# In the steps that clear the bank of sums, the sums go behind the step's other products in TensorE's order

## The chip, the cores and the metric

The kernel runs on one core of a Trainium2 chip. The metric is the device time of one execution in microseconds (us). Before the change three runs took 12238.09, 12265.75 and 12289.24 us; their median is 12265.75 us.

## The reference

Two layers of the same kind follow each other on 8 images of 64 x 64 positions and 96 channels. Each layer normalises its input by groups of three channels, projects it to 192 inner channels, applies a 3 x 3 convolution to each channel and a SiLU, and then runs a state-space scan over the positions in four directions: by rows, by columns, and both backwards. In a direction every channel has 16 states, driven by a step width delta:

```python
dA = jnp.exp(d_t[..., None] * A)
h = dA * h + d_t[..., None] * B_e * u_t[..., None]
return (h, jnp.sum(h * C_e, axis=-1))
```

The four directions are summed, normalised over the channels, gated with a SiLU of a second projection, projected back to 96 channels and added to the layer's input. The second layer writes the same scan with cumulative sums.

## The kernel before

**Tiling of the scan.** The scan of one image is cut into units (4 directions x 4 pieces of 1024 positions), a unit into two jobs (halves of 96 channels), a job into three groups of 32 channels, and a group into four sets of four states, so that a set fills 128 partitions x 1024 positions. One image has 384 such sets, and the main loop of `scan_rows` (L431) goes through them one set a step; each step `n` issues pieces of the work of several sets, ahead of it and behind it. For the second layer most of the scan is left out, and six short sets at the end of an image's loop stand for it. Between the loops of two images stands an output phase.

**One set.** ScalarE (ACT) computes the decay into one of two PSUM tiles (`fill`, L936). VectorE (DVE) multiplies the drive with B (L970) and runs the scan in place (L983). For the last set of each group GpSimd (POOL) makes that product in DVE's place (`early`, L960). POOL multiplies the scanned states with C (`read_out`, L999) into one of four `out` buffers. TensorE (PE) sums the states of each channel (`collect`, L1035): eight matmuls with a 0/1 matrix, which add into the group's bank `acc`. There is one bank, `pacc` having one buffer. For the first set of a group `collect` first clears the bank: it starts the accumulation with the sum so far, read from the map (L1026, eight matmuls), and then adds the eight products. When the fourth set of the group is in, ACT copies the bank back to the map in four pieces (`release`, L1065).

**The order in a step.** The whole loop is under `manual_schedule`, so each engine runs its instructions in the order in which the code emits them. In step `n` the loop emits `advance_set` for set `n`, `keep_state` for `n - 1`, `fill` for `n + 1`, `drive`, `release` for set `n - 4`, `read_out` for set `n - 1`, `early` for set `n + 2`, `collect` for set `n - 3`, and at last the stages that the plan holds for this step. The buffer that `collect` has read in step `n` is written again by the read-out of step `n + 2`. In every fourth step, where `n + 1` is a multiple of 4, `release` empties the bank of one group and `collect` clears it for the next.

**The plan.** It is a dictionary from steps to lists of stages, filled with fixed offsets. A job's offsets count from the step `n = 12 m - 1`, so offsets 0, 4, 8 and 12 fall on the steps that clear the bank. Two users share one PSUM bank, `pmisc`, with a single buffer:

- `ready_by_time` (L673) prepares the step widths delta of the job two ahead: `argument(0)` at offset 0 and `argument(1)` at offset 1 (L690, eight matmuls each, with 7 rows), taken by ACT with `parts` (L701, L702) at offsets 1 and 2; elementwise work at offsets 3 to 7; `total` at offsets 10 and 11 (L724), taken by ACT with `delta` (L736) at offsets 11 and 12; POOL's `product` (L602) at 13, and the stores to DRAM at 14. Offset 12 of one job is offset 0 of the next: there `delta(1)` empties the bank that `argument(0)` takes.
- `conv_beside` (L1068 and on) convolves the next image's maps, one window of 8 rows and 96 channels in a job. `products` (L1102) adds 9 taps, each a pair of matmuls; then ACT's tanh (`curve`, L1112), DVE's `product` (L1115) and a store follow. `windows` (L1163) gives the start and the counts of taps in successive steps: (3, 2, 2, 2) from offset 3 in most jobs, with the tanh at offset 7 and the product at 9; (3, 3, 3) from offset 5 in jobs that also project; (3, 3, 3) from offset 10 in the last two jobs of an image.
- `projection` (L563) of a unit two ahead has its matmuls (L572) at offsets 2 and 3, in every second job of the first two directions.

```python
release(at(-4), y, beside)
gate(at(1))
read_out(at(-1), work)
early(at(2), work)
collect(at(-3), xc, y, pacc)
for stage in plan.pop(n, []):
    stage()
```

Of the kernel before, what the change touches and what calls it, by code (L numbers as in the profile page):

```python
# [29 lines left out]
NS = N // GS  # L30
# [22 lines left out]
def two_ss2d_layers(ctx: ExitStack, tc: tile.TileContext, t: dict, out: bass.AP):  # L53
# [377 lines left out]
    def scan_rows(xc, y, parts, plan, rows, beside):  # L431

        with (
            tc.tile_pool(name="loads", bufs=2, side="right") as loads,
            tc.tile_pool(name="piece", bufs=1) as piece,
            tc.tile_pool(name="work", bufs=2) as work,
            tc.tile_pool(name="pslot", bufs=2, space=PSUM) as pslot,
            tc.tile_pool(name="pdrive", bufs=1, space=PSUM) as pdrive,
            tc.tile_pool(name="pacc", bufs=1, space=PSUM) as pacc,
            tc.tile_pool(name="pmisc", bufs=1, space=PSUM) as pmisc,
        ):  # L450
            units, jobs, sets, x_dbl = parts
            total = len(sets)
            plan = plan(pmisc)
            with tc.manual_schedule():
                state = None
                arena = piece.tile([P, 4 * T], F32, name="arena")
                plan.setdefault(-1, []).insert(0, lambda: low_rows(x_dbl, units[1], rows))
                for n in range(-AHEAD, max(total + 4, max(plan, default=0) + 1)):
                    at = lambda i: sets[n + i] if 0 <= n + i < total else None
                    m, j = divmod(n + 1, PER)  # L460
                    if j == 0 and 0 <= m < len(jobs):

                        stages = []
                        if m + 2 < len(jobs):
                            prepare = short_ready if jobs[m + 2]["unit"]["short"] else ready_by_time
                            stages += prepare(xc, x_dbl, jobs[m + 2], arena, pmisc)
                        if m % NH == 1 and m // NH + 2 < len(units):
                            unit = units[m // NH + 2]
                            project = short_projection if unit["short"] else projection
                            stages += project(xc, x_dbl, unit, rows, pmisc)  # L470
                        for step, stage in stages:
                            plan.setdefault(n + step, []).append(stage)
                    fetch(at(AHEAD), False, loads)
                    fetch(at(2), True, loads)
                    replicate(at(AHEAD_BC), x_dbl, loads)
                    replicate_short(at(AHEAD_BC), "b", loads)
                    replicate_short(at(AHEAD_BC - 1), "c", loads)
                    if at(0) and at(0)["unit"]["nth"] == 0 and at(0)["first"]:
                        state = piece.tile([P, D // GC * NS], F32, name="state0", bufs=2)
                    advance_set(at(0), state, work)  # L480
                    keep_state(at(-1))
                    fill(at(1), pslot)
                    drive(at(2), False, pdrive)
                    drive(at(1), True, pdrive)
                    release(at(-4), y, beside)
                    gate(at(1))
                    read_out(at(-1), work)
                    early(at(2), work)
                    collect(at(-3), xc, y, pacc)
                    for stage in plan.pop(n, []):  # L490
                        stage()
                assert not plan

    def blocks(ap, i):
# [24 lines left out]
    def fetch(s, short, loads):  # L519

        if s and s["i"] == 0 and s["unit"]["short"] == short:
            group, n = s["group"], s["unit"]["n"]
            for c in ("dt", "dtu", "cum") if short else ("dt", "dtu"):
                if c == "cum":
                    rep = loads.tile([P, T], F32, tag="bc_rep", name="cum_rep", bufs=ring(s))
                else:
                    rep = loads.tile([P, T], F32, name=f"{c}_rep")
                group[c] = rep[:, :n]
                src = group["job"][f"{c}_far"][GC * group["g"] :, :][:GC, :]
                nc.sync.dma_start(group[c], src.unsqueeze(1).broadcast_to([GC, GS, n]))  # L530

    def replicate(s, x_dbl, loads):

        if s and s["group"]["h"] == 0 and s["group"]["g"] == 0 and not s["unit"]["short"]:
            unit = s["unit"]
            rows = x_dbl[unit["k"] % 2][unit["k"] // 2 * ROWS :, unit["t0"] : unit["t0"] + T]
            for c, at in (("b", R + 1), ("c", R + 1 + N)):
                rep = loads.tile([P, T], F32, tag="bc_rep", name=f"{c}_rep", bufs=2 * NS + 1)
                src = rows[at + GS * s["i"] :, :][:GS, :]
                nc.sync.dma_start(rep, src.unsqueeze(0).broadcast_to([GC, GS, T]))  # L540
                unit[c, s["i"]] = rep

    def replicate_short(s, c, loads):

        if s and s["unit"]["short"] and s["group"]["h"] == 0 and s["group"]["g"] == 0:
            unit = s["unit"]
            rep = loads.tile([P, T], F32, tag="bc_rep", name=f"{c}_rep", bufs=ring(s))
            unit[c, 0] = rep[:, :HT]
            at = R if c == "b" else R + N
            for i in range(NS):  # L550
                src = blocks(unit["far"][at + GS * i :, :][:GS, :], i)
                nc.sync.dma_start(
                    blocks(unit[c, 0], i), src.unsqueeze(0).broadcast_to([GC, *src.shape])
                )

    def low_rows(x_dbl, unit, piece):

        k, t0 = unit["k"], unit["t0"]
        unit["x_dbl"] = piece.tile([2 * ROWS, T], F32, name="x_dbl0")
        src = x_dbl[k % 2][k // 2 * ROWS :, t0 : t0 + T]  # L560
        nc.sync.dma_start(unit["x_dbl"][: R + 1, :], src[: R + 1, :])
# [387 lines left out]
    def drive(s, short, pdrive):  # L949

        if s and s["i"] == 0 and s["unit"]["short"] == short:
            s["group"]["drive"] = pdrive.tile([P, T], F32, name="drive")[:, : s["unit"]["n"]]
            nc.scalar.copy(s["group"]["drive"], s["group"]["dtu"])  # L953
# [38 lines left out]
    def keep_state(s):  # L992
        if s and not s["unit"]["short"] and s["unit"]["nth"] < NT - 1:
            nc.scalar.copy(s["last"], s["buf"][:, edge(s["unit"])])  # L994
# [6 lines left out]
    def collect(s, xc, y, pacc):  # L1001

        if not s:
            return
        unit, group = s["unit"], s["group"]
        h, g = group["h"], group["g"]
        if s["i"] == 0:
            group["acc"] = pacc.tile([P, MM], F32, name="acc0")
        if unit["short"]:
            for k in range(K):  # L1010
                for i in range(NS):
                    nc.tensor.matmul(  # L1012
                        group["acc"][GC * k : GC * (k + 1), head_of(i, k)],
                        w["gather"],
                        s["out"][:, place(i, k)],
                        start=i == 0,
                        stop=i == NS - 1,
                        skip_group_check=True,
                    )
            return  # L1020
        n = T // Q
        parts = [(group["acc"][GC * a : GC * (a + 1), :n], a * n) for a in range(Q)]
        if s["i"] == 0:
            old, lhs = (xc, w["skip0"][:, h, :]) if unit["k"] == 0 else (y, w["eye"])
            for acc, at in parts:
                nc.tensor.matmul(  # L1026
                    acc,
                    lhs[:, GC * g : GC * (g + 1)],
                    positions(old[:, h, :], unit["column"], unit["t0"] + at, n),
                    start=True,  # L1030
                    stop=False,
                    skip_group_check=True,
                )
        for acc, at in parts:
            nc.tensor.matmul(  # L1035
                acc,
                w["gather"],
                s["out"][:, at : at + n],
                start=False,
                stop=s["i"] == NS - 1,  # L1040
                skip_group_check=True,
            )
# [854 lines left out]
    xc, parts = begin()  # L1897

    with tc.manual_schedule():
        for b in range(NB):  # L1900
            y = keep.tile([C, NH, L], F32, name="map")
# [5 lines left out]
            if b + 1 < NB:  # L1907
                xc, parts = between(b, y)
# [101 lines left out]
```

## Time and profile before

| | |
|---|---|
| profiled execution | 12297.89 us, its span 12296.1 us |
| median of three runs | 12265.75 us |
| mean granted TensorE clock | 0.767 |
| collect L1035, PE | 24576 matmuls, 512 ns mean, 2447.3 us busy |
| clearing L1026, PE | 4608 and 1536 matmuls, 588 and 505 ns; idle before them 1681.6 and 288.3 us |
| release L1065, ACT | 3072 copies, 478 ns |
| taps L1102, PE | 4032 matmuls, 741 ns |
| argument L690, PE | 3840 matmuls, 353 ns |
| delta L736, ACT | 480 copies, 582 ns |
| tanh L1112, ACT | 224, 594 ns; idle before them 278.6 us |
| read-out L999, POOL | 3120, 2364 ns; idle before them 926.3 us |
| scan L983, DVE | 2304 and 768, 2344 and 2285 ns |

The profile is of one execution. "Idle before" is the time in which the engine did nothing directly ahead of the instructions of a row, and the releaser is what ended that time. Matmuls are pipelined, so that the mean length of one is longer than the time that each adds to the engine; the busy sums do not count the overlap twice. In the timeline a row merges equal instructions that follow closely (x8), with the start of the first and the time from there to the end of the last.

### The profile page before, as it was taken

To read this page: it belongs to the slowest core of one execution; us is meant where nothing else is said; L and a number is where in the kernel's file an instruction comes from. 1 tells how busy PE (TensorE), PEld (TensorE's weight loads), DVE (VectorE), ACT (ScalarE), POOL (GpSimd) and SP (SyncE) were. 2 spreads that over 40 slices of the span, in tenths; PEclk is the share of its full clock that TensorE was granted. 3 is DMA by queue.
4 is the path that set the end of the run, shared out by engine and by line. 5 is a ranking of instruction groups with operands and counts; after the bars stand their busy time and mean duration, and the time that the engine had idled before them with its cause. 6 is when DMAs were issued, how large, how long until landed. Compare 5 with 4: busy or idle time off the path is not lost. (4 is left out here: it accounts for less than half of the span.)

```text
span 12296.1 us, 147791 instructions
## 1 busy us (share of the span) xinstructions
PE 9019.4 (73%) x50996; PEld 3932.9 (32%) x50996; DVE 10887.7 (89%) x6819; ACT 9077.6 (74%) x14930; POOL 10481.5 (85%) x4748
## 2 busy tenths in 40 slices
PE   5765577777777777777777777777778776876557
PEld 2332233332333323333233333333333332333222
DVE  6999889997999979998799997999879998799985
ACT  4777767777777777777778777777777777777775
POOL 3999889996899969998699986999869998799983
PEclk8776777778777788777887778777787777877677
DMA  3444444445444444444444445444444445444441
GB/s 97 167 151 156 134 161 153 151 163 152 154 159 162 155 149 167 153 153 157 145 165 163 161 145 156 156 155 161 154 147 165 156 157 163 134 160 160 157 146 58
DMA packets 670708, 1862.42 MB, mean 151 GB/s; under 512 B 186729, under 2 KB 201487, under 8 KB 669950
## 3 DMA queue, kind: packets, MB, share of 16 engines
q1 hardware_dynamic: 662781, 1840.30, 45.1%
q10 hardware_dynamic: 7168, 12.59, 0.3%
q8 instruction: 405, 6.64, 0.2%
q14 instruction: 354, 2.89, 0.1%
HBM read 1539.34 MB, written 313.28 MB: 151 GB/s over the span
## 5 line engine op out<-in xcount | busy, mean ns | idle before, releaser
L999 POOL TENSOR_TENSOR out<-set,c_rep 128x1024 f32<-128x1024 f32 x3120 | 7310.5, 2364 | 926.3 <-PE acc L1035 406.4
L983 DVE TENSOR_TENSOR_SCAN set<-decay,state,set 128x1024 f32<-128x1024 f32 x2304 | 5359.6, 2344 | 451.8 <-ACT decay L936 220.0
L936 ACT ACTIVATE decay<-dt_rep,w_a 128x1024 f32<-128x1024 f32 x3072 | 3423.2, 1115 | 445.4 <-DVE set L983 442.9
L970 DVE TENSOR_TENSOR set<-drive,b_rep 128x1024 f32<-128x1024 f32 x2352 | 2817.1, 1198 | 24.9 <-ACT drive L953 14.4
L1102 PE MATMUL ps_conv<-edged,taps 96*96 96x512 f32 (+1 forms) x4032 | 2426.7, 741 | 34.2 <-DVE arena L862 25.9
L1035 PE MATMUL acc<-out,w_gather 128*32 128x256 f32 x24576 | 2447.3, 512 | 5.1 <-POOL out L999 5.0
L960 POOL TENSOR_TENSOR set<-dtu_rep,b_rep 128x1024 f32<-128x1024 f32 x768 | 1844.4, 2402 | 115.5 <-DMA b_rep<-x_dblr 40.5
L983 DVE TENSOR_TENSOR_SCAN set<-decay,set 128x1024 f32<-128x1024 f32 x768 | 1742.1, 2285 | 160.2 <-ACT decay L936 80.6
L1026 PE MATMUL acc<-map,w_eye 96*32 96x256 f32 x4608 | 581.0, 588 | 1681.6 <-ACT map L1065 1432.5
L724 PE MATMUL ps_sp<-w_eye,arena 128*96 128x128 f32 x7680 | 1161.5, 316 | 635.0 <-ACT arena L736 588.3
L1065 ACT COPY map<-acc 32x256 f32<-32x256 f32 x3072 | 1469.3, 478 | 57.7 <-PE acc L1035 17.5
L724 PEld LDWEIGHTS ps_sp<-w_eye,arena 128*96 128x96 f32 x7680 | 1006.8, 148 | 942.8 <-ACT arena L736 705.3
L1035 PEld LDWEIGHTS acc<-out,w_gather 128*32 128x32 f32 x24576 | 816.2, 137 | 1495.0 <-issue 1084.6
L994 ACT COPY state<-set 128x1 f32<-128x1 f32 x2304 | 433.3, 188 | 1125.7 <-DVE set L983 1116.8
L1102 PEld LDWEIGHTS ps_conv<-edged,taps 96*96 96x96 f32 (+1 forms) x4032 | 725.5, 200 | 1377.7 <-issue 1253.6
L690 PE MATMUL ps_dt<-w_dtw,x_dbl 7*128 7x96 f32 x3840 | 749.9, 353 | 124.5 <-ACT arena L702 60.4
L953 ACT COPY drive<-dtu_rep 128x1024 f32<-128x1024 f32 (+1 forms) x816 | 815.7, 1000 | 27.6 <-DVE x_in L1647 11.2
L690 PEld LDWEIGHTS ps_dt<-w_dtw,x_dbl 7*128 7x128 f32 x3840 | 650.4, 252 | 405.2 <-ACT arena L702 211.0
L1026 PEld LDWEIGHTS acc<-map,w_eye 96*32 96x32 f32 x4608 | 104.5, 125 | 2060.7 <-ACT map L1065 1785.7
L602 POOL TENSOR_TENSOR arena<-arena,map 96x1024 f32<-96x1024 f32 x240 | 632.8, 2637 | 7.1 <-ACT arena L736 7.1
L701 ACT ACTIVATE arena<-ps_dt 128x384 f32<-128x384 f32 x480 | 235.7, 491 | 467.4 <-PE ps_dt L690 445.1
L572 PE MATMUL ps_proj<-map,w_wx 96*78 96x512 f32 x512 | 416.0, 952 | 15.3 <-ACT z L636 9.1
(202 smaller groups left out, 7659.5 us busy)
## 6 DMA issues: line engine op xcount, KB each, us to landing
dt_rep<-dt_far SPq DMA_DIRECT2D x768, 512.0 KB
dtu_rep<-dtu_far SPq DMA_DIRECT2D x768, 512.0 KB
b_rep<-x_dblr SPq DMA_DIRECT2D x256, 512.0 KB
c_rep<-x_dblr SPq DMA_DIRECT2D x256, 512.0 KB
b_rep<-x_dblc SPq DMA_DIRECT2D x256, 512.0 KB
c_rep<-x_dblc SPq DMA_DIRECT2D x256, 512.0 KB
dt_far<-arena SPq DMA_DIRECT2D x240, 384.0 KB
dtu_far<-arena SPq DMA_DIRECT2D x240, 384.0 KB
```

What stands on the lines that cost most here:

```text
L690: nc.tensor.matmul(job["ps"][:, j, :], unit["x_dbl"][: R + 1, at : at + P], w["dtw0"][:, k, h * C : (h + 1) * C], start=True, stop=True,)
L724: nc.tensor.matmul(job["ps"][:C, j * P : (j + 1) * P], job[name][:, s * BLOCKS + j, :], w["whole_eye"], is_transpose=True, start=i == 0, s ...
L936: nc.scalar.activation(s["decay"], s["group"]["dt"], AF.Exp, scale=rate)
L953: nc.scalar.copy(s["group"]["drive"], s["group"]["dtu"])
L960: nc.gpsimd.tensor_tensor(s["buf"], s["group"]["dtu"], b, ALU.mult)
L970: nc.vector.tensor_tensor(s["buf"], s["group"]["drive"], b, ALU.mult)
L983: nc.vector.tensor_tensor_scan(ordered(s["buf"], unit), ordered(s["decay"], unit), ordered(s["buf"], unit), 0.0 if unit["nth"] == 0 else s ...
L999: nc.gpsimd.tensor_tensor(s["out"], s["buf"], s["unit"]["c", s["i"]], ALU.mult)
L1026: nc.tensor.matmul(acc, lhs[:, GC * g : GC * (g + 1)], positions(old[:, h, :], unit["column"], unit["t0"] + at, n), start=True, stop=False ...
L1035: nc.tensor.matmul(acc, w["gather"], s["out"][:, at : at + n], start=False, stop=s["i"] == NS - 1, skip_group_check=True,)
L1065: nc.scalar.copy(yk, like(acc, unit["column"]))
L1102: nc.tensor.matmul(job["ps"][:C, :], taps[l][:k, h, tap, :], edged[:k, tap // 3 : tap // 3 + rows, tap % 3 : tap % 3 + WW], start=tap == 0 ...
```

## The change

In the steps whose `n + 1` is a multiple of `NS` (4), `collect` is emitted behind the plan's stages of that step; in all other steps it stays ahead of them. The instructions and their number are the same.

```diff
@@ -486,9 +486,13 @@
                     gate(at(1))
                     read_out(at(-1), work)
                     early(at(2), work)
-                    collect(at(-3), xc, y, pacc)
+                    late = (n + 1) % NS == 0
+                    if not late:
+                        collect(at(-3), xc, y, pacc)
                     for stage in plan.pop(n, []):
                         stage()
+                    if late:
+                        collect(at(-3), xc, y, pacc)
                 assert not plan
```

## The prediction

> **What bounds the kernel now.** I read the page's busy times first, then the list of waits, then the timeline of single steps; the page's chain of waits follows only the last 0.1 ms and says nothing of the scan.
>
> ```profile
> PE 9019.4 (73%) x50996; PEld 3932.9 (32%) x50996; DVE 10887.7 (89%) x6819; ACT 9077.6 (74%) x14930; POOL 10481.5 (85%) x4748
> ...
> PEclk8776777778777788777887778777787777877677
> ```
>
> DVE (89%) and POOL (85%) pace the scan; TensorE has room on average, but at a clock that is granted at 0.767 over the span (the second line, in tenths).
>
> ```profile
> PE acc L1026 <- ACT map L1065: 1720.8, 555, 14.7
> ...
> ACT arena L701 <- PE ps_dt L690: 445.1, 410, 16.5
> ...
> POOL out L999 <- PE acc L1035: 406.4, 241, 4.8
> ...
> DVE set L983 <- ACT decay L936: 300.5, 147, 11.3
> ...
> ACT conv_out L1112 <- PE ps_conv L1102: 276.3, 100, 8.4
> ```
>
> (Engine and line, for whom it waited: us in all, times, longest.) The 1720.8 us are what the change touches: the clearing sums wait until ACT has copied the bank out. They are idle time of an engine that does not pace. What can be won lies in the last two rows: ACT waits for the convolution before its tanh, ACT is then late with the next decay, and DVE's scan waits for that.
>
> **Which steps change.** A job has 12 steps, j = (n+1) mod 12; j = 4, 8 and 0 are the late ones. By the plan's offsets and TensorE's order in the trace:
> - j = 8: no product stands in the plan (in 14 short jobs the two of L853, whose bank is free before). TensorE's longest wait, 4.06 us on the mean, stays.
> - j = 4: in 158 of the 224 convolution windows (counts 3,2,2,2 from offset 3) two taps now go ahead of the sums. The 54 windows of units that project start at offset 5 and have none there; 12 at the end of the images have three taps in j = 0.
> - j = 0: in 232 jobs the first half of the delta's argument (8 matmuls of L690) goes ahead.
>
> The sums are matmuls alone: no DMA moves, and no other queue is passed.
>
> **j = 4, the gain.** One window, at the half clock:
>
> ```profile
> 4025.41 2.10 PE L1102 MATMUL ps_conv<-edged,taps 96*96 96x512 f32 x4
> ...
> 4029.30 1.49 ACT L1065 COPY map<-acc 32x256 f32<-32x256 f32 x4
> ...
> 4030.84 1.08 PE L1026 MATMUL acc<-map,w_eye 96*32 96x256 f32 x8 [3.33 <-ACT map L1065]
> ...
> 4032.71 3.73 PE L1102 MATMUL ps_conv<-edged,taps 96*96 96x512 f32 x4
> ...
> 4045.81 0.59 ACT L1112 ACTIVATE conv_out<-ps_conv 96x512 f32<-96x512 f32 x1 [4.85 <-PE ps_conv L1102]
> 4046.31 1.10 ACT L936 ACTIVATE decay<-dt_rep,w_a 128x1024 f32<-128x1024 f32 x1
> ...
> 4047.44 2.35 DVE L983 TENSOR_TENSOR_SCAN set<-decay,state,set 128x1024 f32<-128x1024 f32 x1 [3.02 <-ACT decay L936]
> ```
>
> From 4030.84 on TensorE never rests until the last tap, so taps that run in the 3.33 us ahead of it bring the end of the convolution forward by as much, and DVE's 3.02 us before the scan of j = 9 go. Over all 158 windows, laid side by side: wait for the release 1.80 us, two taps 2.73 us (1.96 at the full clock, 3.73 at the half), wait before the tanh 1.60 us, idle of DVE before the scan of j = 9 1.14 us, of which 0.10 us stands before every scan. So at most 1.04 x 158 = 164 us can be won. A window wins the least of four: release wait (less 0.52 us, next part), taps, tanh's wait, scan's idle. Summed over the windows this is 77 us, and nearly all of it lies in the 89 windows whose taps ran mostly at the half clock (0.87 us each; DVE idles 1.90 us there, 0.14 us in the other 69). The 12 late windows: DVE's whole wait for tanh (L1115's row) is 15.1 us, about 8 of it theirs; I take 8.
>
> In the 89 windows 1.90 - 0.10 - 0.87 = 0.93 us stay, unless the clock rises sooner. The trace gives the clock in stretches that are multiples of 3.41 us. If L690's matmuls (7 rows) are left out, a stretch at the full clock with TensorE under 40% busy was followed by half in 395 of 395, one over 60% by full in 98%; at the half clock almost only stretches over 80% were followed by full, in 64%. Taps that close the gap make such a stretch likelier: I take 15 of the 89 windows, 15 x 0.93 = 14 us, between 0 and 83. The Trainium skill (TensorE: Matmul & The Clock Gate, Part 1) says that about 3.4 us of sustained activity open the gate and an idle window closes it; the trace agrees in the length and adds the shares. By that rule alone every closed gap should pay, which is the first rival below.
>
> **j = 4, the cost.** The sums come later by the taps that outlast the release: 1.55 us on the mean with the shift below. POOL's read-out of j = 6 needs the buffer that they free and now comes 1.91 us after them. Window by window POOL would stall 0.66 us, and DVE's scan of j = 8, which takes POOL's product L960, 0.19 us, 30 us in all. But where DVE is late at j = 8 it idles less at j = 9: between 0 and 30, I take 15.
>
> **j = 0, the cost.**
>
> ```profile
> 4058.71 1.49 ACT L1065 COPY map<-acc 32x256 f32<-32x256 f32 x4
> ...
> 4060.22 0.58 ACT L736 COPY arena<-ps_sp 96x512 f32<-96x512 f32 x1
> ...
> 4060.25 0.64 PE L1026 MATMUL acc<-map,w_eye 96*32 96x256 f32 x8 [0.67 <-ACT map L1065]
> ...
> 4061.26 1.13 PE L690 MATMUL ps_dt<-w_dtw,x_dbl 7*128 7x96 f32 x8
> ...
> 4062.42 0.49 ACT L701 ACTIVATE arena<-ps_dt 128x384 f32<-128x384 f32 x1 [0.59 <-PE ps_dt L690]
> ...
> 4065.14 2.38 POOL L999 TENSOR_TENSOR out<-set,c_rep 128x1024 f32<-128x1024 f32 x1
> ```
>
> L690 needs the one bank that ACT's copy L736 empties, and this copy stands behind the four of the release. Now the sums (4060.25) fill the copy's 0.6 us. Afterwards TensorE, in order, waits for the copy, runs L690, then the sums; behind it stand the next sums and the second half of L690. Over the 232 jobs: sums end 2.04 us later, the first half ends 0.78 us sooner, the second starts 0.56 us later. ACT waits less for the first (L701, part of 445.1 us) and more for the second.
>
> What hides this: POOL's read-out of j = 2 comes 2.6 to 3.2 us after the sums, since POOL has just run L602 (2.64 us); the decays are filled about 2 us before their scans. Without cover it would be 232 x 2.04 = 473 us. With it, the jobs whose slack is too small put 15 us (convolution windows) and 6 us (jobs without one) on DVE's scan of j = 4: I take 20. In the 54 windows that project, TensorE is busy through j = 4, so the 0.56 us reach ACT's takes and the scan of j = 6, which already idles 0.37 us there: between 0 and 30, I take 10.
>
> **Sum**: -77 - 8 - 14 + 15 + 20 + 10 = -54 us. The profiled execution took 12297.89 us (span 12296.1), 32 us over the median of the three runs, 12265.75. The same 54 us off the median give 12212 us (-0.44%). About 0.5%, 61 us, is what a measurement of this kernel tells from no change.
>
> **Rivals.**
> 1. The closed gap keeps the clock up in all 89 windows. They then idle like the other 69: 89 x (1.90 - 0.14) = 157 us, with the 8 and the costs of 45 -120 us: **12146 us**. For it: the shares above. Against it: three stretches after 4032.7 were 100% busy and stayed at half; and at j = 0 the wait, the copy and L690 now make 1.5 + 0.6 + 1.1 = 3.2 us in a row that count for nothing.
> 2. The tanh comes sooner and nothing is won: POOL also waits on the release of j = 8 (1.89 us at j = 10), and DVE's idle moves there. Gains 0, costs 45: **12311 us**. Against it: that release stands behind the same tanh on ACT, so both come forward together.
> 3. Slower: POOL's cover at j = 2 is gone. If POOL, freed of its wait at j = 10, is 1 us earlier at j = 2, its slack is 1.6 us against sums that are 2.04 us late: 0.44 x 232 = 102 us, passed on to DVE by L960, whose scan has 0.2 us to spare; and the 0.66 us at j = 6 pass whole, 158 x 0.66 = 104. With 10 and the gains of 99: +117 us, **12383 us**. It decides from a slack below 2.0 us. For it: L960 is already late for 0.4 us of DVE's idle at j = 4. Against it: POOL meets DVE again by j = 0, where it waits 0.36 us for DVE.
>
> That the new order does not take effect is excluded: each engine runs in the order written, and the late condition meets every clearing step of the main loop.
>
> **Chances.** Forecast 0.36 (its own range 12150 to 12270; nearly half of it beyond -61 us: 0.17 faster, 0.19 same), rival 1 0.22 (faster), rival 2 0.15 (same), rival 3 0.27 (0.25 slower, 0.02 same). So faster 0.39, same 0.36, slower 0.25. The range goes from 12120, a little past rival 1, to 12370, nearly rival 3.
>
> **What would show it.** L1026's wait for L1065 falls by some 158 x 1.5 = 240 us at j = 4 and 232 x 1.25 = 290 us at j = 0, where it comes back, with the copy, as 232 x 1.85 = 430 us of L690 waiting for L736; L1112's wait for L1102 falls from 276 to some 180; L983's wait for L936 falls by about 80; L999's wait for L1035 changes by less than 50. If POOL's wait at j = 2 or L983's wait for L960 grows by over 100 us, rival 3 holds; a mean clock above 0.79 speaks for rival 1. I am wrong at the root if L1112's wait stays.

## The result, and the profile after

The changed kernel takes 12188.66 us (median of 6 runs, 12172.82 to 12201.17); the kernel before took 12277.67 us beside it (12238.09 to 12323.45). The ratio is 0.9925, with a 95% interval of 0.9901 to 0.9949: 92 us faster, between 63 and 122. The profiled execution took 12189.28 us, 109 us less than the profiled one of before. All line numbers beyond L493 are four higher than before. First two lines of the page:

```profile
PE 8804.0 (72%) x50996; PEld 4018.9 (33%) x50996; DVE 10891.5 (89%) x6819; ACT 9067.0 (74%) x14930; POOL 10497.4 (86%) x4748
...
PEclk7776677778777887778877778777787777877667
```

The same number of matmuls keeps TensorE busy for 215 us less, which is work at a higher clock; but the row of the granted clock hardly differs, and its mean is 0.770 against 0.767. The clock went up in some steps and down in others, as shown below. The list of waits (engine and line, for whom; us in all, times, longest):

```profile
PE acc L1030 <- ACT map L1069: 1315.4, 268, 12.3
...
ACT arena L705 <- PE ps_dt L694: 597.4, 364, 13.9
...
PE ps_dt L694 <- ACT arena L740: 423.1, 232, 3.1
POOL out L1003 <- PE acc L1039: 329.8, 296, 3.8
...
DVE set L987 <- ACT decay L940: 160.5, 128, 9.4
...
DVE set L987 <- POOL set L964: 97.6, 96, 4.1
...
ACT conv_out L1116 <- PE ps_conv L1106: 27.0, 29, 2.4
```

The last row is the one to look at: ACT's wait before the tanh is nearly gone, from 276.3 to 27.0 us, and DVE's wait for a decay fell by 140 us, from 300.5. The third row is new: TensorE now waits for the copy L740 ahead of the argument, 232 times. The window that the prediction showed, in the timeline of the changed kernel:

```profile
3986.16 7.56 PE L1106 MATMUL ps_conv<-edged,taps 96*96 96x512 f32 x10
...
3990.53 1.49 ACT L1069 COPY map<-acc 32x256 f32<-32x256 f32 x4
...
3993.65 0.64 PE L1030 MATMUL acc<-map,w_eye 96*32 96x256 f32 x8
...
3995.08 1.96 PE L1106 MATMUL ps_conv<-edged,taps 96*96 96x512 f32 x4
...
3997.54 1.96 PE L1106 MATMUL ps_conv<-edged,taps 96*96 96x512 f32 x4
...
4002.21 0.59 ACT L1116 ACTIVATE conv_out<-ps_conv 96x512 f32<-96x512 f32 x1
4002.70 1.10 ACT L940 ACTIVATE decay<-dt_rep,w_a 128x1024 f32<-128x1024 f32 x1
...
4005.76 2.35 DVE L987 TENSOR_TENSOR_SCAN set<-decay,state,set 128x1024 f32<-128x1024 f32 x1
```

The first five taps (x10) run in one piece across the release, so the sums find the bank empty and wait for nothing. And the later taps take 1.96 us where they took 3.73: the clock's record is at full from 3992.27 to 4002.51, where it was at half from 4029.26 to 4046.32 before. The convolution ends at 3999.50 (3997.54 + 1.96), the tanh waits for nothing, and neither does the scan of j = 9 in the last row, which waited 3.02 us before.

Over all 158 such windows, from the first tap to the last: 16.01 us before, 12.92 after. Of the 3.09 us, 1.38 are idle time that is filled (1.80 to 0.42), 1.08 are shorter taps (11.26 to 10.18) and 0.63 shorter sums (2.95 to 2.32). DVE's idle before the scan of j = 9 fell from 1.14 to 0.14 us, the 0.10 us of every scan included. What was given back: 0.07 us before the scan of j = 4 in these windows, 0.23 us a job in the 54 that project, 0.13 in the 32 without a window. The eight main loops together are 117.6 us shorter (10453.8 to 10336.2); what lies between them is 9 us longer in this execution.

### The profile page after: what moved, and what is told of

The parts are those of the page before. It is cut to its first block, busy times and chain, and to the rows that moved or that the text cites. A ratio compares the mean times of both kernels' runs of the same rounds, so it can differ in the third digit from the quotient of the medians.

```text
span 12187.5 us, 147673 instructions
## 1 busy us (share of the span) xinstructions
PE 8804.0 (72%) x50996; PEld 4018.9 (33%) x50996; DVE 10891.5 (89%) x6819; ACT 9067.0 (74%) x14930; POOL 10497.4 (86%) x4748
## 5 line engine op out<-in xcount | busy, mean ns | idle before, releaser
L1039 PE MATMUL acc<-out,w_gather 128*32 128x256 f32 x24576 | 2384.5, 516 | 6.8 <-POOL out L1003 6.7
L1106 PE MATMUL ps_conv<-edged,taps 96*96 96x512 f32 (+1 forms) x4032 | 2198.5, 688 | 10.9 <-ACT arena L706 8.3
L1039 PEld LDWEIGHTS acc<-out,w_gather 128*32 128x32 f32 x24576 | 878.3, 140 | 1382.9 <-issue 1072.0
L694 PE MATMUL ps_dt<-w_dtw,x_dbl 7*128 7x96 f32 x3840 | 798.1, 370 | 498.7 <-ACT arena L740 423.1
L694 PEld LDWEIGHTS ps_dt<-w_dtw,x_dbl 7*128 7x128 f32 x3840 | 695.3, 267 | 743.6 <-ACT arena L740 496.6
```

Source lines behind the costliest of these rows:

```text
L694: nc.tensor.matmul(job["ps"][:, j, :], unit["x_dbl"][: R + 1, at : at + P], w["dtw0"][:, k, h * C : (h + 1) * C], start=True, stop=True,)
L1039: nc.tensor.matmul(acc, w["gather"], s["out"][:, at : at + n], start=False, stop=s["i"] == NS - 1, skip_group_check=True,)
L1106: nc.tensor.matmul(job["ps"][:C, :], taps[l][:k, h, tap, :], edged[:k, tap // 3 : tap // 3 + rows, tap % 3 : tap % 3 + WW], start=tap == 0 ...
```

## The experiments

Two theories were open after this. **A**: the gain is made at j = 4 alone, by the filled wait and by the clock, and the argument that goes ahead at j = 0 costs some of it back. **B**: both steps are needed, since the argument that comes sooner helps ACT. Within A it was open how much the clock carries.

**Each late step alone.**

```diff
-                    late = (n + 1) % NS == 0
+                    late = (n + 1) % PER == 4
```

This is the edit for j = 4; `PER` is 12, the steps of a job, and the other two kernels have 0 and 8 in place of the 4.

> The sums go behind only in the steps j = 4, where two taps of the convolution go ahead; j = 0 and j = 8 stay as before. Theory A (the gain is made at j = 4, and the argument ahead at j = 0 costs some 20 to 30 us): faster than before by 110 to 135 us, a ratio near 0.990, DVE's wait for the decay below 160 us, L690's wait for the copy L736 back near nothing. Theory B (the gain needs both, since the argument that comes sooner helps ACT): faster by less than 60 us.

> The sums go behind only in the steps j = 0, where the first half of the delta's argument goes ahead. Theory A: slower than before by 15 to 40 us, a ratio of 1.001 to 1.003; DVE's wait for POOL's product L960 up by some 15 us, the scan of j = 6 in the jobs that project later by 0.2 us, the tanh's wait no shorter than 276 us. Theory B: faster by 20 us or more.

> The sums go behind only at j = 8, where the plan holds no product on TensorE but in 14 short jobs. Every theory expects no change: within 15 us of before, a ratio within 0.002 of 1. It also shows what the measurement makes of no change.

| late at | median us | ratio to before | 95% interval |
|---|---|---|---|
| j = 4 | 12143.22 | 0.9895 | 0.9874 to 0.9916 |
| j = 0 | 12326.37 | 1.0052 | 1.0032 to 1.0073 |
| j = 8 | 12274.98 | 0.9982 | 0.9966 to 0.9998 |

A holds and B falls: j = 4 alone wins 131 us, and as expected DVE's wait for the decay is below 160 us there (153.2) and L690's wait for the copy is gone. j = 0 alone costs 53 to 64 us, more than the 15 to 40 expected. The list of waits with j = 0 alone:

```profile
PE ps_dt L694 <- ACT arena L740: 442.0, 232, 3.1
...
DVE set L987 <- ACT decay L940: 330.8, 200, 10.8
...
ACT conv_out L1116 <- PE ps_conv L1106: 260.7, 94, 8.3
...
DVE set L987 <- POOL set L964: 101.3, 114, 3.6
```

The first row is the wait for the copy, against the 1.85 us each that were forecast (430 us). The second and the last are 30 and 17 us above before; the tanh's wait is 16 us shorter, where no shorter one was expected. By steps, DVE idles 0.15 us a job more in the 158 windows (24 us, of which 19 stand before the scan of j = 4), and 0.37 us more in the 54 that project (20 us), where the prediction took 10 us.

The steps j = 8 were expected to do nothing. The measured gain is 2 to 42 us, at the edge of what the runs can tell, and a measure of how far to trust the small differences below. In its profile the two taps at j = 4, which this kernel does not touch, ran at the half clock (a mean granted clock below 0.6 while they run) in 23% of the windows, against 31% in the profile of before, and DVE idles 0.79 us before the scan of j = 9, against 1.14. The runs of the kernel before themselves spread from 12231.92 to 12328.67 us over the batches, those of the change and of j = 4 alone from 12113.62 to 12201.17. I read it as the clock, which the trace shows falling differently in the two executions, but no run isolates that.

**The clock without the gain of time.** The order of before, and in the 158 windows two taps of zeros run ahead of the clearing sums at j = 4. They add nothing to the result and save no work.

```diff
+        def nothing(job):
+            for _ in range(2):
+                nc.tensor.matmul(
+                    job["ps"][:C, :],
+                    zeros[:C, :],
+                    edged[:C, 1 : 1 + rows, 1 : 1 + WW],
+                    start=False,
+                    stop=False,
+                    skip_group_check=True,
+                )
...
+                if len(counts) == 4:
+                    fillers[step + 1] = [lambda job=job: nothing(job)]
...
+                    for stage in fillers.pop(n, []):
+                        stage()
                     collect(at(-3), xc, y, pacc)
```

The second run has `zeros[:7, :]` and `edged[:7, ...]` in their place.

> The order of before, but in the 158 windows two taps with a matrix of zeros (96 rows, so nothing is added to the result) run ahead of the clearing sums at j = 4; the real taps stay behind the sums. So the wait is filled and no work is saved. If the clock carries a good part of the gain: the real taps at j = 4 to 6 run at the full clock in nearly all windows, the time from the first tap to the last of a window falls below the 16.0 us of before in spite of the longer queue, and the kernel is faster than before by 30 to 100 us. If only the filled time counts: no faster, or slower by up to 40 us, since the sums come later where the zero taps outlast the release.

> As the run with zero taps of 96 rows, but the zero matmuls use 7 rows only, like those of the delta's argument; they take as long. If the clock goes by the work of matmuls and 7 rows count for nothing, as the stretches of the clock in the trace of before suggest: the real taps stay at the half clock as often as before, and the kernel is slower than before by 10 to 60 us. If any matmul keeps the clock up: the same as with 96 rows.

With 96 rows: 12225.03 us, ratio 0.9958 (0.9942 to 0.9974), 52 us faster. With 7 rows: 12509.14 us, ratio 1.0185 (1.0159 to 1.0212), 227 us slower. Three rows of the list of waits, first with 96 rows, then with 7 (L1107 and L1128 are the taps and the tanh, L1102 and L1112 before; L941, L988, L1004 and L1040 stand five further down than before):

```profile
POOL out L1004 <- PE acc L1040: 379.8, 221, 4.8
...
DVE set L988 <- ACT decay L941: 247.3, 132, 11.1
...
ACT conv_out L1128 <- PE ps_conv L1107: 183.2, 75, 6.8
```

```profile
POOL out L1004 <- PE acc L1040: 669.7, 313, 5.3
...
ACT conv_out L1128 <- PE ps_conv L1107: 542.6, 130, 11.4
...
DVE set L988 <- ACT decay L941: 525.8, 194, 11.2
```

Two kernels with the same queue, and 284 us between them. The rows of the zero matmuls themselves differ little:

```profile
L1117 PE MATMUL ps_conv<-edged,zeros 96*96 96x512 f32 x632 | 303.8, 602 | 0.0
```

```profile
L1117 PE MATMUL ps_conv<-edged,zeros 7*96 7x512 f32 x632 | 346.6, 670 | 0.0
```

That is 0.48 and 0.55 us of TensorE each, or 0.27 us over the four of a window. What differs is what comes behind them: the nine real taps of a window take 10.32 us after zeros on 96 rows, 11.26 before, and 12.29 after zeros on 7 rows. The granted clock by step, from the clock's record, mean over the 158 jobs with the early window:

| kernel | j = 3 | 4 | 5 | 6 | 7 | taps us | tanh's wait us |
|---|---|---|---|---|---|---|---|
| before | 0.65 | 0.77 | 0.74 | 0.86 | 0.90 | 11.26 | 1.60 |
| change | 0.60 | 0.74 | 0.91 | 0.97 | 0.95 | 10.18 | 0.19 |
| j = 4 alone | 0.62 | 0.84 | 0.93 | 0.98 | 0.94 | 9.87 | 0.06 |
| zeros, 96 rows | 0.68 | 0.88 | 0.89 | 0.94 | 0.95 | 10.32 | 1.00 |
| zeros, 7 rows | 0.65 | 0.78 | 0.70 | 0.72 | 0.79 | 12.29 | 3.27 |

So matmuls of no use are worth 52 us when they keep the clock up, though they lengthen the queue. The 52 us are only twice what j = 8 alone showed; the 284 us between the two kernels are far beyond it. Real taps in their place (j = 4 alone, 131 us) add the filled time. The 7-row run was expected to lose 10 to 60 us and lost 227: with those matmuls the clock is lower than with an idle gap (0.72 against 0.86 at j = 6). I take it that the real taps come later still behind work that hardly counts; no run tests this.

**One tap ahead instead of two**, the other behind the sums, as before at j = 0 and 8:

```diff
+                    if len(counts) == 4 and first == 3:
+                        ahead[step] = [lambda job=job, c=c, h=h: products(job, c, h, 3, 1)]
+                        put(step, products, job, c, h, 4, 1)
...
+                    for stage in ahead.pop(n, []):
+                        stage()
                     collect(at(-3), xc, y, pacc)
```

> At j = 4 one of the two taps goes ahead of the sums and one stays behind; j = 0 and j = 8 as before. If filled time is all that counts, a tap of 0.49 us (full clock) to 0.93 us (half) wins at most that in a window: some 40 us. With the clock, which rises sooner on the longer run of taps, more than half of the 130 us that both taps won when moved alone: 65 to 100 us faster than before, and the taps behind the sums at the half clock in fewer windows than before, in more than with both taps ahead.

12160.92 us, ratio 0.9883 (0.9862 to 0.9904): 144 us, as much as with two taps and more than expected. The 40 us for filled time were too few: a tap is two matmuls and takes 0.98 to 1.87 us (half of the 1.96 and 3.73 of two taps), and the least of release wait, one tap, tanh's wait and scan's idle, summed over the windows, is 72 us. 144 is still twice that. No window's taps of j = 4 ran at the half clock, as with two; the tanh's wait is 0.30 us and DVE's idle before the scan of j = 9 is 0.23. The gain is not in proportion to the taps that move; with one tap too the clock stays up behind the wait (0.91 at j = 5, against 0.74 before).

**Rows of the argument.** With only j = 4 late, the argument's matmuls use 39 rows in place of 7, with added weights of zero:

```diff
-                    unit["x_dbl"][: R + 1, at : at + P],
-                    w["dtw0"][:, k, h * C : (h + 1) * C],
+                    unit["x_dbl"][:ROWS, at : at + P],
+                    wide[:, k, h * C : (h + 1) * C],
```

> The order in which only j = 4 is late (12143 us), and the argument's matmuls of the main loop use 39 rows in place of 7, the added rows with weights of zero, so the result stays; the low rows are loaded with 39 rows too. If TensorE's work at 7 rows counts for nothing and at 39 rows counts: the granted clock at j = 1 to 3, now 0.74, 0.62, 0.62 in the jobs with the early window, rises by 0.1 or more, L690's matmuls get shorter, the 54 jobs that project idle less before the scan of j = 6, and the kernel is 10 to 40 us faster than with j = 4 alone. If rows make no difference to the clock: within 15 us of it, and the clock there as before.

12151.69 us, ratio 0.9875 (0.9855 to 0.9896). The clock does rise, at j = 1, 2 and 3 from 0.74, 0.62 and 0.62 to 0.77, 0.71 and 0.72, and L690's matmuls go from 361 to 346 ns. The time does not follow, where 10 to 40 us less than with j = 4 alone (0.9895) were expected: the jobs that project idle before the scan of j = 6 as before (0.46 against 0.45 us).

The last batch asked whether j = 0 costs because of the clock or because of the order, with four kernels side by side:

> All late steps as in the change (j = 0, 4 and 8), with the argument's matmuls on 39 rows (added weights of zero). What does the argument ahead of the sums cost at j = 0, where it put 20 to 50 us on the time? If it is the clock (the wait, the copy and 7-row matmuls in one idle stretch): the cost goes with 39 rows, and this runs within 15 us of j = 4 alone with 39 rows in the same batch. If it is the order (TensorE idle until the copy L736 has emptied the bank, so that the second half of the argument comes later): it stays 20 to 50 us slower than j = 4 alone with 39 rows.

> The change itself, in the same batch: 0.990 to 0.995 of before. With j = 4 alone beside it, the difference is the cost of j = 0 with 7 rows: 20 to 50 us.

> Only j = 4 late, 7 rows, in the same batch: 0.987 to 0.992 of before, 20 to 50 us faster than the change.

> Only j = 4 late, 39 rows, in the same batch: within 15 us of j = 4 alone with 7 rows, since the clock at j = 1 to 3, which the rows do raise, ends no wait of DVE there.

| late steps | argument on 7 rows | on 39 rows |
|---|---|---|
| j = 0, 4, 8 | 12170.17 us, 0.9913 (0.9895 to 0.9931) | 12172.01 us, 0.9920 (0.9902 to 0.9938) |
| j = 4 | 12132.34 us, 0.9889 (0.9869 to 0.9910) | 12156.30 us, 0.9904 (0.9885 to 0.9923) |

With 7 rows j = 0 costs 38 us, with 39 rows 16 us, which is neither of the two outcomes expected; each ratio is known to 0.2%, 25 us, so the two costs are not clearly apart. The profiles show the order at work: before the scans of j = 4 DVE idles 37 us more with j = 0 late on 7 rows, and 25 us more on 39 (TensorE waits 420 and 415 us for the copy). Whether the clock is another part stays open. With j = 4 alone the 39 rows are 24 us slower, where at most 15 were expected, and that too is within the noise. j = 4 alone with 7 rows is the fastest of all, 38 us ahead of the change in this batch.

## Why the prediction was right

**The bound and the place of the gain** were right: DVE's idle before the scan of j = 9, behind decay, tanh and taps, at j = 4. It was 1.04 us above every scan's 0.10 and is now 0.04, so 158 us went, all but a few of the 164 that could go.

**The size of the clock's term was wrong.** The sum had 77 us for the filled wait (taken window by window again, the least of its four comes to 84) and 14 us for a clock that rises sooner in 15 of the 89 windows at the half clock. It rises in far more of them. The prediction's 89 are the windows whose mean granted clock during the two taps is below 0.75; 24 such windows are left after the change, and of the 49 (31%) below 0.6 none is left. In the 24 DVE idles 0.14 us before the scan of j = 9, like in the others. The two terms came to 91 us and measured 158 between the two profiles. A part of the 158 may belong to the execution that was profiled before the change: it took 20 us more than the median of the six runs of before, and with j = 8 alone, whose windows keep the order of before, the same idle is 55 us less. What the prediction gave as its first rival is nearly what happened in the windows. Against it stood three stretches at 100% that stayed at half, and why they did is open: in the changed kernel too 204 of the 734 stretches of 3.41 us at the half clock in which TensorE is over 80% busy (L690 left out) are followed by half, against 330 of 928 before.

**The time alone shows little.** The range of 12120 to 12370 us held the first rival's 12146 as well. The 89 us between the medians lie between the forecast's 54 and the rival's 120, and nothing in them tells the filled wait from the clock. That is told by the idle before the scan of j = 9, by j = 4 alone and by the matmuls of zeros.

**The marker for that rival was wrong too.** A mean clock above 0.79 was to show it. The mean is 0.770: in the jobs with an early window steps 5 to 7 gained up to 0.17, while j = 0 to 4 lost 0.03 to 0.05 each and j = 8 lost 0.08, where TensorE, done sooner, waits longer for the release (4.07 to 4.63 us on the mean of all jobs).

**The rule of the Trainium skill** (TensorE: Matmul & The Clock Gate, Part 1: sustained activity opens the gate, an idle window closes it) pointed the right way and further than the forecast did. The 7-row run shows its limit here: with matmuls that fill the time as well, 121 of the 158 windows have their two taps below 0.75, against 89 before and 31 with zeros on 96 rows.

**The costs.** By DVE's idle the scan of j = 4 took 11 us in the windows and 4 us in the jobs without one, where 20 were forecast. The scan of j = 8 took 4 us in place of 15: as the clock rose, the taps no longer outlast the release by much. The jobs that project took 12 us, forecast 10. The late windows gained their 8 us ahead of DVE's product (L1115), but their jobs lost 11 us in other places, so that they took 3. That makes 34 us, where the forecast had 45 us of costs and a gain of 8. 158 - 34 = 124 us stand against 117.6 us in the loops and 92 us in the measurement.

**That the cost before the scan of j = 4 looks small is luck.** With j = 4 alone late, DVE idles 17 us less before that scan in the windows than before (0.41 in place of 0.51 us), and its wait for POOL's L960 is 63.5 us in place of 84.3. The forecast had no such gain. Against j = 4 alone, the change's 11 us are 28. So j = 0 costs more than the forecast's 20 + 10 us: 53 to 64 us alone, 38 us on top of j = 4.

**The other markers.** L1026's wait fell by 405 us. By steps, TensorE's idle before it fell by 219 us at j = 4 in the 158 windows and by 293 at j = 0 in the 232 jobs, as forecast (240 and 290), and grew by 143 us at j = 8, which was not. L690 waits 423 us for the copy (430). The tanh's wait fell to 27 us, not to 180; DVE's for decays by 140, not 80. POOL's wait for the sums fell by 77 us, where less than 50 was forecast. L960 is late for 13 us more, so **rival 3** (POOL's cover gone) did not come, although the slack at j = 2 shrank from 2.7 to 0.7 us. **Rival 2** is refuted by j = 4 alone: the 159 us of idle before the scan of j = 9 went, and before the scans of no other step did DVE's idle grow by more than 5 us.

## What to carry to other kernels

An engine that does not pace can still set the time through its clock: before work is moved, look at which clock the matmuls around the gap run at, and whether the move closes the gap or opens another. Put ahead of a wait only what is ready: the taps were, and won 131 us; the argument had a wait of its own and gave 38 to 64 us back. A gain that comes through the clock is not in proportion to what is moved, and the mean clock of the whole span does not show it: it is 0.788 in the run with zeros on 96 rows, which won 52 us, and 0.775 with j = 4 alone, which won 131. Read it by step.

## What the hardware showed that was not expected

- The clock record's stretches are multiples of 3.41 us. In these runs TensorE's busy time counts towards the clock by what its matmuls are: two zero taps on 96 rows brought the clock at j = 5 from 0.74 to 0.89, the same two on 7 rows to 0.70, at 0.48 and 0.55 us a matmul. 39 rows in the argument in place of 7 raised the clock behind it, at j = 2 and 3, from 0.62 to 0.71 and 0.72.
- Matmuls of pure zeros, with a queue that is longer by two taps in each of 158 windows, made the kernel 52 us faster.
- Runs of the order that keeps the clock up also agree better: 12172.82 to 12201.17 us for the change against 12238.09 to 12323.45 for before in the same batch.
